# The second layer's M moved into the first attention, and softmax denominators by transposes, in a two-layer graph attention kernel on one core

## The chip, the cores and the metric

The kernel runs on one core of a Trainium2 chip. Its engines, as the profile names them, are PE (TensorE, matmuls and transposes; its weight loads are listed as PEld), DVE (VectorE), ACT (ScalarE), POOL (GpSimd) and SP (SyncE, which here only issues DMAs). The metric is the time of one execution in device microseconds; the time shown for a kernel is a median of its runs. The profile is that of one execution, and its own time is given beside its span.

## The reference, cut to what matters

`x` has 3327 rows of 512 features, `adj` is a 3327 x 3327 matrix of zeros and ones. There are two attention layers, then a layer with binary weights, each closed by a residual and a layer norm:

```
for l in range(2):                      # W_stack[l] is 512 x 1024
    Wh, Ws = split(x @ W_stack[l])
    a = softmax(Wh @ Ws.T) * adj
    x = leaky_relu(a @ Wh + x)
x = layernorm(x0 + x)
out = layernorm(x + relu(adj @ (step(x) @ sign(weight).T)))
```

The scores are `x Wa (x Wb)^T = x (Wa Wb^T) x^T`, where Wa and Wb are the left and the right half of W. The kernel makes the 512 x 512 matrix of the two halves once per layer and calls it M, so that Ws is never formed: queries are x times M, keys are x itself. M depends on the weights alone.

## The kernel before, in words

The 3327 rows are 26 tiles of 128. Two tiles make a half (13 halves, `NQ`), four make a chunk (7 chunks). Large products are done in seven smaller products with sums of operands before and sums of results after (the Strassen and Winograd scheme, `seven`), so each product comes with VectorE, ScalarE and POOL additions. All matmuls are in 32-bit floats, and each shows as two records in the profile.

Each layer has two stages. **`project`** transposes the rows of x, builds M, writes the keys, the values (`ws_d`, with `wh` kept on the chip) and the queries (`gs_d`) with their operand sums to memory. For M it loads the left half of W as `wa` and the right half as `wb`, transposes all sixteen 128 x 128 blocks of each half on TensorE (`pwT`, copied out to `wTs`), and then multiplies them (`pm`, four bands of four matmuls, copied out to `m`). `weave` mixes M's 16 matmuls with the products of the first two value tiles (`wh`). The products for the first queries need M and its sums `msum`.

**`attention`** runs over 169 steps, one for each pair (half of queries `g`, half of keys `q`). In the loop over `v` a step issues, in an order set by fractions from 0 to 1: the scores of 30 steps ahead (`LOOK`, `scores`), the exponentials and running sums of 3 and 2 steps ahead, POOL's operand sums of the masked weights (`sums`, tiles `as`), and the seven value products of step `v` (`values`). The scores of the last chunk have only one half and take less work; from step 152 on no scores are left, and only values are multiplied. After the last step of a half, `finish` adds its parts over the next steps, one per step: `norm` makes the denominators, then residuals and activation follow.

In `norm`, the running total of the exponentials lies with keys on partitions; it is summed over the partitions by a matmul with a column of ones:

```
nc.tensor.matmul(pz[:, i : i + 1], sm[:, ts(i, P)], ones[:, 0:1], start=True, stop=True)
nc.vector.reciprocal(rz, pz)
```

What sets the order: each engine has its own queue and works it in order. Within a stage the order is that in which the program calls the operations; where two stages meet, operations of the next one may be placed between those of the one before. SP's queue holds nearly all loads, in order; POOL's queue holds the stores to memory besides POOL's own sums. Buffers are rings: `slot` gives the next of 33 tiles of 2 KB per partition, used for scores, rows of x, W and operand sums alike; accumulators come from PSUM pools `ps_ch` (3 banks, scores), `ps_acc` (4, values) and `ps_tr` (1, transposes and denominators).

At the start of the second attention `binary_weights` loads the weights of the last layer (`wT`) and makes their signs on VectorE (`neg_w`, `bw`). Their buffers are those of the last rows of x1 (`h`), so the loads wait until these rows are stored. In VectorE's queue they stand among the operations of the second `project`.

Of the kernel before, what the change touches and what calls it, by code (L numbers as in the profile page):

```python
# [9 lines left out]
F32 = mybir.dt.float32  # L10
# [6 lines left out]
AX = mybir.AxisListType  # L17
PSUM = bass.MemoryType.PSUM

P = 128  # L20
# [9 lines left out]
def kernel(  # L30
# [8 lines left out]
    nc = tc.nc  # L39
    N, D = x.shape  # L40
    L = w_stack.shape[0]
    KD = D // P
    HD = D // 2
# [75 lines left out]
    def copy_out(n, dst, src):  # L119
        if n % 2:  # L120
            nc.scalar.copy(dst, src)
        else:
            nc.vector.tensor_copy(dst, src)
# [55 lines left out]
    def left_sums(a11, a12, a21, a22, s1, s2, s3, s4):  # L179
        nc.vector.tensor_tensor(s1, a21, a22, ALU.add)  # L180
        nc.vector.tensor_tensor(s2, s1, a11, ALU.subtract)
        nc.vector.tensor_tensor(s3, a11, a21, ALU.subtract)
        nc.vector.tensor_tensor(s4, a12, s2, ALU.subtract)
# [7 lines left out]
    def weave(*lists):  # L191

        at = [
            ((i + 0.5) / len(part), n, do)
            for n, part in enumerate(lists) for i, do in enumerate(part)
        ]
        for _, _, do in sorted(at, key=lambda e: e[:2]):
            do()

    def project(l, pre):  # L200

        src = x if l == 0 else x1_d
        ch_lane, acc_lane, tr_lane = (ps_ch, "ch"), (ps_acc, "acc"), (ps_tr, "tr")
        xTs, rows_of = {}, {}

        def load_x(c):
# [28 lines left out]
        wb = []  # L235
        for k in range(KD):
            wt = slot([P, D], F32, f"wb_{l}_{k}")
            nc.sync.dma_start(out=wt, in_=w_stack[l, ts(k, P), D:])
            wb.append(wt)
        load_x(1)  # L240
        for k in range(KD):
            transpose_x(0, k, acc_lane)
        wT = {}
        for h in range(2):
            for k in range(KD):
                pool, tag = (acc_lane, ch_lane)[h]
                pt = pool.tile([P, D], F32, tag=tag, name=f"pwT_{l}_{h}_{k}")
                for d in range(KD):
                    of = wa[:, d] if h == 0 else wb[d]
                    nc.tensor.transpose(pt[:, ts(d, P)], of[:, ts(k, P)], ident)  # L250
                wT[h, k] = slot([P, D], F32, f"wTs_{l}_{h}_{k}")
                copy_out(k, wT[h, k], pt)
# [6 lines left out]
        wr = {B11: lo[:, :, :HD], B21: hi[:, :, :HD], B22: hi[:, :, HD:]}  # L259
        wr.update({i: wsum[:, e] for e, i in enumerate((T1, T2, T3, T4))})  # L260
        m = pre.tile([P, KD, D], F32, tag="m", bufs=1, name=f"m_{l}")
        msum = pre.tile([P, 4, 2, HD], F32, tag="msum", bufs=1, name=f"msum_{l}")
        lo, hi = m[:, 0:2], m[:, 2:4]
        ml = {A11: lo[:, :, :HD], A12: hi[:, :, :HD], A21: lo[:, :, HD:], A22: hi[:, :, HD:]}
        ml.update({i: msum[:, e] for e, i in enumerate((S1, S2, S3, S4))})

        def product_m():
            pm = {}

            def one(d, k):  # L270
                if k == 0:
                    pm[d] = ps_acc.tile([P, D], F32, tag="acc", name=f"pm_{l}_{d}")
                nc.tensor.matmul(  # L273
                    pm[d], wT[0, k][:, ts(d, P)], wT[1, k], start=(k == 0), stop=(k == KD - 1)
                )
                if k == KD - 1:
                    copy_out(d, m[:, d], pm[d])

            return [lambda d=d, k=k: one(d, k) for d in range(KD) for k in range(KD)]

        def keys(c, a):

# [128 lines left out]
    def attention(l, att):  # L411
        last = l == L - 1
# [305 lines left out]
        def finish(g):  # L718

            sm = total[g][:, 0]  # L720
            nc.gpsimd.tensor_tensor(sm, sm, total[g][:, 1], ALU.add)
            pz = ps_tr.tile([P, 2], F32, tag="tr", name=f"pz_{l}_{g}")
            rz = small.tile([P, 2], F32, tag="rz", name=f"rz_{l}_{g}")
            hs = out_.pop(g)
            mine = half_tiles(g)
            held = {}

            def norm():
                for i in range(2):
                    nc.tensor.matmul(  # L730
                        pz[:, i : i + 1], sm[:, ts(i, P)], ones[:, 0:1], start=True, stop=True
                    )
# [24 lines left out]
            def sign(i):  # L757

                t, hh = mine[i], hs[i]
                r = rows(t)  # L760
                st = small.tile([P, 6], F32, tag="bn", name=f"bn_{t}")
                nc.vector.bn_stats(st[:r], hh[:r])
                nc.vector.bn_aggr(mv[:r, t, :], st[:r])
                ba = held[i] = att.tile([P, D], BF16, tag="ba", bufs=1, name=f"ba_{t}")
                nc.vector.tensor_scalar(ba[:r], hh[:r], mv[:r, t, 0:1], None, ALU.is_gt)

            def turn(i):
                r = rows(mine[i])
# [24 lines left out]
            if not last:  # L793
                return [norm, lambda: (residual(0), fetch(1)), lambda: None, lambda: residual(1)]
            return [
                norm, lambda: (residual(0), fetch(1)), lambda: sign(0), lambda: turn(0),
                lambda: linear(0), lambda: residual(1), lambda: sign(1), lambda: turn(1),
                lambda: linear(1),
            ]

        if last:
            binary_weights()
        later, after = [], []
        for v in range(-LOOK - 4, len(steps)):
            u = v + LOOK
# [200 lines left out]
```

## Time and profile before

| what | value |
|---|---|
| median of 3 runs | 2721.83 us (2717.41 to 2726.82) |
| the profiled execution, its own time | 2719.29 us |
| its span | 2717.4 us |
| PE, DVE, POOL, ACT busy | 98%, 69%, 48%, 24% of the span |
| mean granted TensorE clock | 0.994 |
| last scores of the first attention end | about 1188 us |
| last value matmul of the first attention ends | 1257.6 us |
| first query product of layer 1 that needs M's sums starts | 1302.22 us |

Times in the profile count from the start of the span. A group of instructions is listed by its source line, its engine, and by what it writes and reads. A line such as "PE a L1 <- DMA b: 2.1, 2, 1.8" in a list of waits says that PE's instructions of line L1, which write a, waited 2.1 us in all, twice, at most 1.8 us, until a DMA into b had landed. In a table of stretches each engine's busy time stands with its number of instructions, then the granted clock as a share of the full one, the busy share of the DMA engines and what they moved.

### The profile page before, as it was taken

The page shows a single profiled execution, that of the slowest core. Times are in us where ns is not written, and L with a number is a line of the kernel's source. Part 1 is how long each engine was busy: PE and PEld are TensorE (multiplying, and loading weights), DVE is VectorE, ACT ScalarE, POOL GpSimd, SP SyncE. Part 2 cuts the span into 40 slices and gives each one's busy share as a digit, 9 for nine tenths or more (in the row PEclk, how much of TensorE's full clock was granted, in tenths as well). Part 3 has the DMA queues.
Part 4 walks back from the last instruction along what each step waited for, and adds up shares of the span by engine and source line. Part 5 has one row for each costly group of instructions (what it writes and reads, how often), then busy time and mean ns, then how long its engine had stood idle before and what let it go on. Part 6 is the DMA issues. An engine that isn't in the chain of part 4 may idle for free.

```text
span 2717.4 us, 38059 instructions
## 1 busy us (share of the span) xinstructions
PE 2651.7 (98%) x12409; PEld 2233.5 (82%) x12409; DVE 1877.1 (69%) x3511; ACT 665.2 (24%) x1571; POOL 1313.6 (48%) x2170
## 2 busy tenths in 40 slices
PE   9999999999999999998999999999999999998997
PEld 6888888888888888876888888888888888877543
DVE  5654777777777777786664667777677777778543
ACT  2323222222222222211332322222222222222100
POOL 2450455555555555775452154545545455566401
PEclk9999999999999999999999999999999999999999
DMA  5765777676777767776665667777777777687882
GB/s 191 258 208 161 237 233 257 226 260 233 257 238 235 260 227 240 254 260 220 235 206 178 206 224 261 239 248 255 238 252 237 275 236 242 235 274 255 286 284 92
DMA packets 280817, 639.54 MB, mean 235 GB/s; under 512 B 35921, under 2 KB 128735, under 8 KB 279078
## 3 DMA queue, kind: packets, MB, share of 16 engines
q1 hardware_dynamic: 244038, 527.32, 58.7%
q0 software_dynamic: 36576, 109.73, 11.0%
q8 instruction: 102, 1.67, 0.2%
q14 instruction: 101, 0.83, 0.1%
HBM read 527.22 MB, written 109.69 MB: 234 GB/s over the span
## 4 chain that ended last, share of the span: by engine, by line
PE 85%; issue 6%; DMA 4%; POOL 3%; DVE 2%; SPq 0%; ACT 0%; POOLq 0%; DVEq 0%; ACTq 0%
PE acc L682 34%; PE pZ L441 19%; PE pY L441 10%; PE pX L441 5%; PE pZ_wh L309 3%; PE pD L441 3%; PE pZ_g L363 3%; DMA ws<-ws_d 2%; PE pY_wh L309 2%; PE pY_g L363 2%; PE pm L273 1%; PE pxw L781 1%; PE pxt L221 1%; PE pX_wh L309 1%; PE pX_g L363 1%
## 5 line engine op out<-in xcount | busy, mean ns | idle before, releaser
L441 PE MATMUL pZ<-gs,xs 128*128 128x256 f32 x2496 | 635.8, 379 | 0.0
L441 PEld LDWEIGHTS pZ<-gs,xs 128*128 128x128 f32 x2496 | 473.6, 190 | 64.8 <-ACT u L458 0.3
L655 POOL TENSOR_TENSOR as<-s 128x128 f32<-128x128 f32 x338 | 168.4, 498 | 734.1 <-DVE s L600 577.1
L682 PE MATMUL acc<-ws,s 128*128 128x256 f32 x1352 | 404.3, 381 | 0.0
L682 PE MATMUL acc<-ws,as 128*128 128x256 f32 x1352 | 352.7, 382 | 30.0 <-DMA ws<-ws_d 17.4
L682 PE MATMUL acc<-wh,s 128*128 128x256 f32 x1352 | 356.9, 380 | 1.7 <-DVE h L706 1.7
L441 PE MATMUL pY<-gs,xs 128*128 128x256 f32 x1248 | 320.3, 379 | 0.0
L511 DVE TENSOR_TENSOR top<-top,s 128x512 f32<-128x512 f32 x312 | 252.7, 810 | 97.8 <-ACT s L493 58.2
L682 PEld LDWEIGHTS acc<-ws,as 128*128 128x128 f32 x1352 | 253.6, 190 | 75.0 <-POOL as L657 12.8
L682 PEld LDWEIGHTS acc<-wh,s 128*128 128x128 f32 x1352 | 258.0, 191 | 37.5 <-DVE h L706 2.1
L682 PEld LDWEIGHTS acc<-ws,s 128*128 128x128 f32 x1352 | 257.3, 191 | 35.1 <-DVE h L714 0.2
L582 DVE TENSOR_TENSOR s<-s,off 128x512 f32<-128x512 f32 x338 | 273.0, 808 | 0.1
L483 DVE TENSOR_TENSOR s<-p,u 128x256 f32<-128x256 f32 x156 | 67.5, 433 | 286.2 <-ACT u L458 285.3
L441 PEld LDWEIGHTS pY<-gs,xs 128*128 128x128 f32 x1248 | 237.0, 190 | 32.3
L585 ACT ACTIVATE s<-s 128x512 f32<-128x512 f32 x338 | 213.7, 632 | 201.5 <-DVE s L582 200.5
L593 DVE TENSOR_TENSOR total<-total,s 128x512 f32<-128x512 f32 x312 | 259.3, 831 | 0.8 <-ACT s L585 0.8
L657 POOL TENSOR_TENSOR as<-s 128x128 f32<-128x128 f32 x338 | 236.5, 700 | 26.5
L600 DVE TENSOR_TENSOR s<-s,adj 128x512 f32<-128x512 f32 (+1 forms) x312 | 226.1, 725 | 5.7
L458 ACT COPY u<-pZ 128x256 f32<-128x256 f32 x312 | 116.4, 373 | 459.9 <-PE pZ L441 459.9
L656 POOL TENSOR_TENSOR s<-s 128x128 f32<-128x128 f32 x338 | 215.2, 637 | 26.5
L658 POOL TENSOR_TENSOR as<-s,as 128x128 f32<-128x128 f32 x338 | 210.5, 623 | 26.5
L682 PE MATMUL acc<-wh,as 128*128 128x256 f32 x676 | 205.8, 386 | 0.0
(185 smaller groups left out, 3501.1 us busy)
## 6 DMA issues: line engine op xcount, KB each, us to landing
ws<-ws_d SPq DMA_DIRECT2D x338, 512.0 KB, 3.9
xs<-xs_d SPq DMA_DIRECT2D x182, 512.0 KB, 5.9
adj<-in_adjT_dram SPq DMA_DIRECT2D x288, 256.0 KB, 4.4
xs<-xs_d SPq DMA_DIRECT2D x156, 384.0 KB, 6.3
gs_d<-gsp POOLq DMA_DIRECT2D x88, 256.0 KB, 3.2
gs<-gs_d SPq DMA_DIRECT2D x12, 1792.0 KB, 11.0
adj_d<-ah POOLq DMA_DIRECT2D x144, 128.0 KB, 4.4
ahl<-adj_d SPq DMA_DIRECT2D x72, 256.0 KB, 4.4
```

The lines of the kernel that those rows point to most:

```text
L309: nc.tensor.matmul(bank, of[LEFT[i]][:, k], wr[RIGHT[i]][:, k], start=(start and k == 0), stop=(k == 1), skip_group_check=True,)
L441: nc.tensor.matmul(ch[bank], xs[c, q, a][:, k], gs[c][:, b, k], start=(start and k == 0), stop=(k == 1), skip_group_check=True,)
L511: nc.vector.tensor_tensor(top[i], top[i], t, ALU.max)
L582: nc.vector.tensor_tensor(s, s, off[g].to_broadcast([P, 2, HW]), ALU.subtract)
L585: nc.scalar.activation(sc[g, q], sc[g, q], AF.Exp)
L593: nc.vector.tensor_tensor(total[g], total[g], sc[g, q], ALU.add)
L600: nc.vector.tensor_tensor(s[:, :, :n], s[:, :, :n], at[:, :, :n], ALU.mult)
L655: nc.gpsimd.tensor_tensor(s3, a11, a21, ALU.subtract)
L656: nc.gpsimd.tensor_tensor(a21, a21, a22, ALU.add)
L657: nc.gpsimd.tensor_tensor(s2, a21, a11, ALU.subtract)
L658: nc.gpsimd.tensor_tensor(s4, a12, s2, ALU.subtract)
L682: nc.tensor.matmul(acc[g][i // 2][:, i % 2], a[i], b[i], start=(q == 0 and i % 2 == 0), stop=(q == NQ - 1), skip_group_check=True,)
```

## The change

For layer 1, W is loaded, transposed and multiplied to M in the last steps of the first attention; layer 0 does as before. Counting steps as `v`: the left half is loaded at step 138 and the right half at 140 into eight slots; in each of the steps 146 to 153 one group of four transposes goes through the `ps_tr` bank and is copied out to a slot; from step 154 to 168 the sixteen matmuls of M run between the value products, in `ps_ch` banks, and are copied out, in turn on VectorE and ScalarE, into two tiles of the ring that held the keys' operands (`xs0`). In the second `project` the left half is still loaded as `wa` for the values; the loads of `wb`, the transposes and M's matmuls are gone. The two value tiles that were woven with M are woven with each other, in `ps_ch` and `ps_acc`. M is copied into its place `m` by two copies on ScalarE, and its sums are made from the tiles of the ring.

In `norm` of both layers the totals are transposed, and the sums are then made by a VectorE reduction along the free axis, and inverted.

```
+    def load_w(l, h):
+        for k in range(KD):
+            w_rows[l, h, k] = slot([P, D], F32, f"w{h}_{l}_{k}")
+            nc.sync.dma_start(out=w_rows[l, h, k], in_=w_stack[l, ts(k, P), ts(h, D)])
+
+    def transpose_w(l, h, k, lane):
+        pool, tag = lane
+        pt = pool.tile([P, D], F32, tag=tag, name=f"pwT_{l}_{h}_{k}")
+        for d in range(KD):
+            nc.tensor.transpose(pt[:, ts(d, P)], w_rows[l, h, d][:, ts(k, P)], ident)
+        wT[l, h, k] = slot([P, D], F32, f"wTs_{l}_{h}_{k}")
+        copy_out(k, wT[l, h, k], pt)
+
+    def product_m(l, lane):
...
+            nc.tensor.matmul(
+                pm[d], wT[l, 0, k][:, ts(d, P)], wT[l, 1, k], start=(k == 0), stop=(k == KD - 1)
+            )
+            if k == KD - 1:
+                copy_out(d, m_of[l][d // 2][:, d % 2], pm[d])
...
-        first, second = (project_values(0, a, ch_lane) for a in range(2))
-        weave(product_m(), first + second)
-        left_sums(*(ml[i] for i in (A11, A12, A21, A22, S1, S2, S3, S4)))
+        if l == 0:
+            first, second = (project_values(0, a, ch_lane) for a in range(2))
+            weave(product_m(l, acc_lane), first + second)
+        else:
+            first, second = (
+                project_values(0, a, lane) for a, lane in enumerate((ch_lane, acc_lane))
+            )
+            weave(first, second)
+            for e in range(2):
+                nc.scalar.copy(m[:, 2 * e : 2 * e + 2], m_of[l][e])
+        of = left(*m_of[l])
+        left_sums(*(of[i] for i in (A11, A12, A21, A22, S1, S2, S3, S4)))
...
-            pz = ps_tr.tile([P, 2], F32, tag="tr", name=f"pz_{l}_{g}")
+            pz = ps_tr.tile([P, 2, P], F32, tag="tr", name=f"pz_{l}_{g}")
...
-                    nc.tensor.matmul(
-                        pz[:, i : i + 1], sm[:, ts(i, P)], ones[:, 0:1], start=True, stop=True
-                    )
-                nc.vector.reciprocal(rz, pz)
+                    nc.tensor.transpose(pz[:, i], sm[:, ts(i, P)], ident)
+                nc.vector.reduce_sum(rz, pz, axis=AX.X)
+                nc.vector.reciprocal(rz, rz)
...
         if last:
             binary_weights()
+        else:
+            end = len(ahead) - LOOK
+            early = {}
+            for h in range(2):
+                early[end - 14 + 2 * h] = [(0.9, lambda h=h: load_w(l + 1, h))]
+                for k in range(KD):
+                    early[end - 6 + KD * h + k] = [
+                        (0.75, lambda h=h, k=k: transpose_w(l + 1, h, k, tr_lane))
+                    ]
...
+            n = len(steps) - end - 2
+            early[end + 2] = [(0.2, begin_m)]
+            for i, do in enumerate(product_m(l + 1, ch_lane)):
+                early.setdefault(end + 2 + i * n // (KD * KD), []).append(
+                    (0.3 + 0.4 * (i % 2), do)
+                )
...
             if v >= 0:
                 work += values(*steps[v])
+            if not last:
+                work += early.get(v, [])
```

More of the change, by code (lines that the diff above doesn't have):

```diff
@@ L198, in weave, with one @@
             do()
+    ch_lane, acc_lane, tr_lane = (ps_ch, "ch"), (ps_acc, "acc"), (ps_tr, "tr")
+    w_rows, wT, m_of = {}, {}, {}
+    def load_w(l, h):
[10 more added lines that the diff above has]
+    def product_m(l, lane):
+        pm = {}
+        def one(d, k):
+            if k == 0:
+                pool, tag = lane
+                pm[d] = pool.tile([P, D], F32, tag=tag, name=f"pm_{l}_{d}")
+            nc.tensor.matmul(
[3 more added lines that the diff above has]
+                copy_out(d, m_of[l][d // 2][:, d % 2], pm[d])
+        return [lambda d=d, k=k: one(d, k) for d in range(KD) for k in range(KD)]
     def project(l, pre):
         src = x if l == 0 else x1_d
-        ch_lane, acc_lane, tr_lane = (ps_ch, "ch"), (ps_acc, "acc"), (ps_tr, "tr")
         xTs, rows_of = {}, {}
@@ L234, in project @@
             nc.sync.dma_start(out=wa[:, k], in_=w_stack[l, ts(k, P), :D])
[L235 to L239, printed above, removed]
+        if l == 0:
+            load_w(l, 1)
+            for k in range(KD):
+                w_rows[l, 0, k] = wa[:, k]
         load_x(1)
@@ L242, in project @@
             transpose_x(0, k, acc_lane)
[L243 to L252, printed above, removed]
+        if l == 0:
+            for h in range(2):
+                for k in range(KD):
+                    transpose_w(l, h, k, (acc_lane, ch_lane)[h])
         wsum = ops.tile([P, 4, 2, HD], F32, tag="gs", name=f"wsum_{l}")
@@ L261, in project, with left @@
         m = pre.tile([P, KD, D], F32, tag="m", bufs=1, name=f"m_{l}")
+        if l == 0:
+            m_of[l] = [m[:, 0:2], m[:, 2:4]]
         msum = pre.tile([P, 4, 2, HD], F32, tag="msum", bufs=1, name=f"msum_{l}")
[L263 to L272, printed above, removed]
-                nc.tensor.matmul(
-                    pm[d], wT[0, k][:, ts(d, P)], wT[1, k], start=(k == 0), stop=(k == KD - 1)
-                )
-                if k == KD - 1:
-                    copy_out(d, m[:, d], pm[d])
-            return [lambda d=d, k=k: one(d, k) for d in range(KD) for k in range(KD)]
+        def left(lo, hi):
+            of = {A11: lo[:, :, :HD], A12: hi[:, :, :HD], A21: lo[:, :, HD:], A22: hi[:, :, HD:]}
+            of.update({i: msum[:, e] for e, i in enumerate((S1, S2, S3, S4))})
+            return of
+        ml = left(m[:, 0:2], m[:, 2:4])
         def keys(c, a):
@@ L379, in queries @@
             return [sums] + one, two + [done]
-        first, second = (project_values(0, a, ch_lane) for a in range(2))
-        weave(product_m(), first + second)
-        left_sums(*(ml[i] for i in (A11, A12, A21, A22, S1, S2, S3, S4)))
+        if l == 0:
+            first, second = (project_values(0, a, ch_lane) for a in range(2))
[9 more added lines that the diff above has]
+        left_sums(*(of[i] for i in (A11, A12, A21, A22, S1, S2, S3, S4)))
         for c in range(NC):
@@ L729, in norm @@
                 for i in range(2):
-                    nc.tensor.matmul(
-                        pz[:, i : i + 1], sm[:, ts(i, P)], ones[:, 0:1], start=True, stop=True
-                    )
-                nc.vector.reciprocal(rz, pz)
+                    nc.tensor.transpose(pz[:, i], sm[:, ts(i, P)], ident)
+                nc.vector.reduce_sum(rz, pz, axis=AX.X)
+                nc.vector.reciprocal(rz, rz)
             def fetch(i):
@@ L802, in attention, with begin_m @@
             binary_weights()
+        else:
+            end = len(ahead) - LOOK
+            early = {}
+            for h in range(2):
+                early[end - 14 + 2 * h] = [(0.9, lambda h=h: load_w(l + 1, h))]
+                for k in range(KD):
+                    early[end - 6 + KD * h + k] = [
+                        (0.75, lambda h=h, k=k: transpose_w(l + 1, h, k, tr_lane))
+                    ]
+            def begin_m():
+                m_of[l + 1] = [
+                    ops.tile([P, 2, D], F32, tag="xs0", name=f"m{e}_{l + 1}") for e in range(2)
+                ]
+            n = len(steps) - end - 2
[4 more added lines that the diff above has]
+                )
         later, after = [], []
```

## The prediction

> **What bounds the kernel now.** I read the page first: its span is 2717.4 us, the profiled execution's own time 2719.29 us, so 1.9 us lie around the span; the median of the three runs, 2721.83 us, stands 2.5 us above that execution. The sum below is made against 2719.3 and carried to 2721.8.
>
> ```profile
> PE 2651.7 (98%) x12409; PEld 2233.5 (82%) x12409; DVE 1877.1 (69%) x3511; ACT 665.2 (24%) x1571; POOL 1313.6 (48%) x2170
> ```
>
> TensorE is the bound on average, but the change works at one place, so next the table of stretches, columns PE, PEld, DVE, ACT, POOL busy, granted clock, DMA share, GB/s. I cut at 1188 (the last scores of the first attention), 1258 (its end) and 1304 (the second projection has got going).
>
> ```profile
> 0.00:1188.00 1188.00, 1177.82 (x5511) 1028.17 (x5512) 837.79 (x1549) 305.15 (x730) 607.41 (x1006) 1.00 0.70 235
> 1188.00:1258.00 70.00, 57.87 (x254) 46.43 (x253) 52.86 (x107) 9.46 (x16) 55.00 (x86) 0.98 0.69 223
> 1258.00:1304.00 46.00, 40.01 (x162) 28.03 (x163) 29.58 (x60) 9.53 (x21) 11.87 (x19) 0.93 0.62 216
> 1304.00:2640.00 1336.00, 1313.12 (x6197) 1101.56 (x6198) 926.01 (x1724) 338.10 (x792) 631.98 (x1046) 1.00 0.73 244
> ```
>
> The first and fourth stretches are TensorE without holes: what is taken off TensorE there is time. In the second it idles 12.1 us. The waits of PE from 1188 to 1258 (in all us, times, longest):
>
> ```profile
> PE acc L682 <- POOL as L657: 9.6, 7, 3.2
> PE acc L682 <- DVE h L706: 1.7, 1, 1.7
> ```
>
> and from 1258 to 1304:
>
> ```profile
> PE pwT L250 <- DMA wa<-in_w_stack_dram: 2.1, 2, 1.8
> PE pZ_wh L309 <- DVE s L181: 1.4, 1, 1.4
> PE pwT L250 <- DMA wb<-in_w_stack_dram: 1.0, 1, 1.0
> PE pZ_g L363 <- DVE xt L187: 0.9, 1, 0.9
> PE pxt L221 <- DVE xT L123: 0.6, 1, 0.6
> ```
>
> So the tail of the first attention (steps 152 to 168, values without scores) waits for POOL's sums of the weights: a step costs 3.03 us of matmuls but comes every 3.9 to 4.1 us. In POOL's timeline from 1192 to 1256 one instruction follows the other, but for 3.0 us at 1242.8 and under 2 us of short gaps. Then the transition: W loads, 32 transposes, M, values, all in series.
>
> **What the Trainium skill says.** "SBUF — State Buffer", Who interferes with whom: a VectorE instruction with two SBUF inputs contends with a GpSimd one that reads SBUF; one with at most one SBUF input outside the two-port modes does not, and a reduce never does. The trace agrees on the first: POOL's 128x128 sums take 0.45 us while VectorE is idle and 0.78 beside its adds. The moved copies and the new reduce read PSUM, so I charge POOL nothing. "TensorE: Matmul & The Clock Gate", What's actually happening: after an idle window of about 3.4 us the clock halves. Here the stretch 1250–1275 has clock 0.86, and its 13 last W transposes took 3.12 us where 13 earlier took 2.18.
>
> **The change, part by part.** Times are relative to E, the end of the last value matmul, 1257.6 before.
>
> 1. Denominators. From the timeline of PE (start, us, x records):
>
> ```profile
> 376.94 0.50 PE L730 MATMUL pz<-ones,total 128*128 128x1 f32 x4
> 377.30 0.68 PE L682 MATMUL acc<-wh,as 128*128 128x256 f32 x2
> 377.82 0.59 PE L682 MATMUL acc<-ws,s 128*128 128x256 f32 x2
> ...
> 1189.70 0.38 PE L543 MATMUL ptop<-ident,top 128*128 128x128 f32 x2
> 1189.92 0.60 PE L682 MATMUL acc<-ws,as 128*128 128x256 f32 x2
> ```
>
> From 376.94 to 377.82 pass 0.88 us for the pz records and one pair that costs 0.43: pz takes 0.44. Two transposes take 0.22 (1189.70 to 1189.92). Gain 0.22 each; 11 of the 13 in each layer lie in TensorE-bound steps: −2.4 us in layer 0, −2.4 in layer 1. VectorE gains a reduce of 128x256 from PSUM, 0.42 us as ptop's (L546), hidden under 70% busy; without that cover it costs 26 × 0.42 = 10.9.
>
> 2. Eight loads of W (256 KB each) on SP's queue, four at step 138, four at 140, ahead of the next ws, adj and xs loads. Each waits for the DMA eight places back and for score copies some eight steps old, so SP isn't held. The first four x1 row loads of layer 1 move about three steps back in the same queue and are still some 14 steps early; POOL's queue is passed by nothing. Transfers: around there a step of 4.75 us moves about 243 GB/s, and peaks of 369 are seen, so 0.6 MB per step is free; 1 MB leaves 0.4 MB, 1.1 us, before the next ws load. ws lands in 3.6/4.2/5.7 us (min/median/max) and is needed 6.2 us after its issue. Cost 0, bound 2.
>
> 3. 32 transposes, one group of four in each of steps 146 to 153. A group costs 0.43 us; 146 to 151 are TensorE-bound (4.75 us a step, no hole): 6 × 0.43 = +2.6. The groups of 152 and 153 fall where POOL has a lead. All pass through the only tr bank: poff at step 152 comes behind a VectorE copy (0.69), about 1 us on off, while POOL reaches those sums 2.9 us after they are ready. Cost 0, bound 1.
>
> 4. M's 16 matmuls, two records each with 0.43 between starts, 0.86 us, in steps 154 to 168: 13.8 us on TensorE against 12.1 us of holes; per step 3.03 + 0.92 = 3.95, just POOL's pace. POOL's "as" tiles have three buffers, so its step and TensorE's overlap. Following POOL's times of before from step 166 (1248.22): 166 ends at 1251.2, 167 with one M matmul at 1255.1, 168 has its sums at 1255.33 and ends, with the last M matmul, at 1259.0: +1.4. Two M copies and two wT copies join VectorE's queue (0.69 each); the M copies stand ahead of the shift of a later step, wait for TensorE, and POOL's sums wait behind; slack there is 1.2 us, 1 to 2 us come in: +0.5, bound 0 to 3. E moves by −2.4 + 2.6 + 1.4 + 0.5 = +2.1.
>
> 5. The transition. Removed: 32 transposes, 8 copies, 16 matmuls, 1 MB of W right-half loads. Kept: wa and wsum. Added: two ScalarE copies of M, 128x1024. Price: "VectorE: DVE Perf Modes", TRN2 errata, gives ScalarE 224 + elements cycles at 1.2 GHz, an estimate of 1.04 us; the exponentials of 512 by the same rule 0.61, measured 0.633. Before, the first query product that needs msum and xt starts at 1302.22 = E + 44.6. After, TensorE: wa lands at about E + 4, values start, stall once for wsum and keys (E + 8.5), end by E + 17.6; the first M copy delays the first query to E + 19.3; with four query products and one transpose group it stands before msum at E + 23.2. VectorE's queue is longer: take-outs to 1.1, reduce, xT copies, residuals and wsum (0.6 each) to 7.7, eight key sums (0.34) to 10.5, two adds to 11.2. Then come the binary weights (neg_w, bw), which stay on VectorE and wait (VectorE's waits from 1258 to 1304):
>
> ```profile
> DVE neg_w L406 <- DMA wT<-in_weightT_dram: 3.0, 2, 2.1
> ```
>
> The wT loads wait for the stores of the last x1 rows (issued about E + 5.4, 4.7 us to landing as a median, 6.1 to 9.1 at this place), then 2.8 us: first at 13.2 to 14.8, third only after the first bw: 17.1 to 18.8. Adds, bw and t sums stand behind; t ends at 23.6 to 25.2, msum and xt (six at 0.62) at 27.4 to 29.1. I take 28. TensorE then idles 4.8 us, long enough for the half clock: +1.2. So E + 29.2 against E + 44.6: −15.4. Where the stall goes: from W loads to VectorE's binary weights. Behind that product the order is the same as before.
>
> Sum: −2.4 + 2.6 + 1.9 − 15.4 − 2.4 = −15.7. 2719.3 − 15.7 = 2703.6; on the median 2706.
>
> **Rivals.** B: VectorE isn't late (x1 stores land fast, clock stays): the product starts at E + 23.2, another −6.0: 2700. For it: the 1 MB of loads that slowed those stores is gone. Against: the third wT load still waits for the first bw. C: the tail hides nothing, M's 13.8 us all come on E instead of 1.4: +12.4, 2718.5, the same as before. For it: 13.8 us into 12.1 us of holes, and VectorE, POOL and TensorE wait for each other in a ring. Against: the three buffers. D, slower: the clock gate, in the tail. There TensorE gets 45.5 + 13.8 = 59.3 us of work; a share of it that runs at half clock takes twice its time, and no hole is left to take it. It turns the gain of 15.7 into a loss of over 8 once it adds 24 us, that is from 40% of the tail on; with 50% it adds 29.7 and gives 2736. For it: a patch of slow matmuls stands at 1205–1209 before, after holes of 1.7 and 0.5, and "TensorE: Matmul & The Clock Gate", Part 4, says that transposes don't keep the clock up. Against: the granted clock is 0.98 over the tail with holes of up to 3.2, the change fills holes, and only two groups of transposes lie there. F: the transposes with a sum don't help (the reduce's latency eats it): 4.8 us less, 2711.
>
> **How the numbers follow.** Chances: forecast 0.58, B 0.12, F 0.10, C 0.14, D 0.06. 0.3% is 8.2 us, about what a measurement of this kernel can tell from no change. Faster by more: 0.55 of the forecast, 0.12 of B, 0.10 of F: 0.77. Same: C with 0.13 and 0.03 of the forecast: 0.16. Slower: D and a rest of C: 0.07. The forecast's own range: better by 3 if POOL's hole of 3.0 at 1242.8 doesn't come back and by 2 from early stores, worse by 3 (tail copies), 2 (burst of loads), 1 (tr bank), 1: 2701 to 2713. With B, F and the near half of C: 2698 to 2717.
>
> **What would show it.** Right: pz pairs of 0.22; no holes in steps 138 to 151; PE's wait for "as" in the tail mostly gone and the end of the values at about 1259.7; no wait for wb; neg_w's wait for wT grown, and a PE wait of some 5 us on xt before the query products. Wrong: waits for ws near step 139 or 141; tail steps over 4.5 us; the query products at E + 23; a clock under 0.9 in the tail.

## The result and the profile after

The changed kernel takes 2706.90 us as a median of five runs (2704.40 to 2711.31); the kernel before, in the same comparison, 2719.62 us (2716.64 to 2726.82). The ratio is 0.9951 with a 95% interval of 0.9933 to 0.9970, which is 8 to 18 us less. The forecast was 2706, in a range of 2698 to 2717. The profiled execution of the changed kernel is the slowest of its five: its own time is 2711.31 us, its span 2709.5 us, so the two profiled executions differ by 8.0 us where the medians differ by 12.7.

The page of the changed kernel, busy time by engine:

```profile
PE 2642.3 (98%) x12332; PEld 2225.7 (82%) x12357; DVE 1884.0 (70%) x3537; ACT 666.5 (25%) x1573; POOL 1312.7 (48%) x2170
```

TensorE is busy 9.4 us less. Only some 6 us of that are work, the 52 records of pz that are gone; 25 more matmul records are missing from this trace, as the count beside PEld's shows. M is the same work in another place. The table of stretches, cut at the same times as before (columns PE, PEld, DVE, ACT, POOL busy, granted clock, DMA share, GB/s), shows where it went:

```profile
0.00:1188.00 1188.00, 1176.24 (x5505) 1026.01 (x5506) 842.67 (x1562) 305.66 (x731) 600.50 (x1005) 1.00 0.70 236
1188.00:1258.00 70.00, 66.36 (x282) 51.03 (x281) 53.20 (x106) 11.10 (x19) 54.95 (x88) 1.00 0.71 225
1258.00:1304.00 46.00, 35.93 (x167) 29.15 (x166) 32.77 (x70) 13.01 (x29) 13.60 (x23) 0.93 0.60 207
1304.00:2640.00 1336.00, 1308.81 (x6128) 1093.80 (x6152) 926.96 (x1731) 333.78 (x782) 636.59 (x1044) 0.99 0.73 246
```

In the second stretch TensorE is busy 66.4 of 70 us in place of 57.9: M went into the holes. The granted clock there is 1.00. In the third it is *less* busy than before, 35.9 of 46 us: the work left, and a new wait came. TensorE's waits from 1188 to 1258:

```profile
PE acc L708 <- POOL as L683: 2.6, 2, 1.8
PE poff L579 <- DVE wTs L123: 0.5, 1, 0.5
PE pz L756 <- POOL total L747: 0.3, 1, 0.3
PE acc L708 <- DMA ws<-ws_d: 0.3, 1, 0.3
```

and from 1258 to 1304:

```profile
PE pZ_g L380 <- DVE xt L187: 5.7, 1, 5.7
PE pZ_wh L326 <- DVE s L181: 1.7, 2, 1.3
PE pZ_g L380 <- ACT m L407: 1.4, 1, 1.4
PE pZ_wh L326 <- DMA wa<-in_w_stack_dram: 0.7, 1, 0.7
PE pX_wh L326 <- DMA wa<-in_w_stack_dram: 0.6, 1, 0.6
```

The waits for wb and for transposed W are gone; one wait of 5.7 us stands in their place, for `xt`, which is VectorE. What held VectorE is in its own list of waits over the same stretch:

```profile
DVE neg_w L432 <- DMA wT<-in_weightT_dram: 5.5, 2, 2.8
```

This is the chain that the prediction describes: binary weights wait for their loads, and M's sums and the query operand sums stand behind them. In TensorE's timeline (start, us, instruction, idle time before it and what ended it):

```profile
1280.88 1.13 PE L380 MATMUL pZ_g<-xT,m 128*128 128x256 f32 x4 [1.41 <-ACT m L407]
...
1283.15 1.89 PE L380 MATMUL pX_g<-xT,m 128*128 128x256 f32 x8
1290.77 2.05 PE L380 MATMUL pZ_g<-xt,msum 128*128 128x256 f32 x4 [5.73 <-DVE xt L187]
```

The last value product ends at 1261.10 (1257.59 before), so the first product with M's sums comes 29.7 us after it, in place of 44.6. Its first four records take 1.83 us to the next start where 0.86 is the rule: the half clock behind the wait, which was forecast. From 1290.77 to 1294.2 the granted clock is 0.50. The product's eight records and the group of transposes among them are through at 1294.71, 3.94 us after its start; where no wait stands before it, in e8, the same work takes 2.16. So the half clock costs 1.8 us, behind the product's start.

The denominators, in TensorE's timeline at the same place as before:

```profile
377.44 0.38 PE L756 MATMUL pz<-ident,total 128*128 128x128 f32 x2
377.66 0.60 PE L708 MATMUL acc<-wh,as 128*128 128x256 f32 x2
```

Two transposes hold TensorE for 0.22 us (0.44 before). To see where along the run time is won and lost, take the start of the exponentials of each step in ScalarE's timeline, changed kernel minus before: +0.5 at the first step, then a drop of 0.2 every thirteen steps to −2.6 at step 143, −2.3 at 144, +2.1 at 154, +2.3 at 168. With the points above: +3.5 at the end of the values, −11.5 at the first product with M's sums. In the second attention −10.6 at its first step, −9.1 at its last, −8.0 at the end.

### The profile page after: what moved, and what is told of

The parts are those of the page before. It is cut to its first block, busy times and chain, and to the rows that moved or that the text cites. A ratio compares the mean times of both kernels' runs of the same rounds, so it can differ in the third digit from the quotient of the medians.

```text
span 2709.5 us, 37972 instructions
## 1 busy us (share of the span) xinstructions
PE 2642.3 (98%) x12332; PEld 2225.7 (82%) x12357; DVE 1884.0 (70%) x3537; ACT 666.5 (25%) x1573; POOL 1312.7 (48%) x2170
## 4 chain that ended last, share of the span: by engine, by line
PE 84%; issue 6%; DMA 4%; DVE 3%; POOL 3%; SPq 0%; ACT 0%; POOLq 0%; DVEq 0%; ACTq 0%
PE acc L708 34%; PE pZ L467 19%; PE pY L467 10%; PE pX L467 5%; PE pZ_g L380 3%; PE pZ_wh L326 3%; PE pD L467 3%; DMA ws<-ws_d 2%; PE pY_wh L326 2%; PE pY_g L380 2%; PE pm L225 1%; PE pX_wh L326 1%; PE pxw L806 1%; PE pxt L253 1%; PE pX_g L380 1%
## 5 line engine op out<-in xcount | busy, mean ns | idle before, releaser
L681 POOL TENSOR_TENSOR as<-s 128x128 f32<-128x128 f32 x338 | 168.1, 497 | 742.6 <-DVE s L626 580.7
L683 POOL TENSOR_TENSOR as<-s 128x128 f32<-128x128 f32 x338 | 230.6, 682 | 26.5
```

Source lines behind the costliest of these rows:

```text
L681: nc.gpsimd.tensor_tensor(s3, a11, a21, ALU.subtract)
L683: nc.gpsimd.tensor_tensor(s2, a21, a11, ALU.subtract)
```

## The experiments

"E" is the end of the last value product of the first attention in the profiled execution, read as the start of what TensorE does next; "product" is the first query product of layer 1 with M's sums. Each ratio is against the kernel before on the same chip (medians there 2718.7 to 2720.0). e1 to e4, e5 to e8 and e9 to e11 each shared a chip, so a difference between rows of different groups carries about a microsecond more of doubt than its medians show.

| run | median us | ratio, 95% interval | E | product − E |
|---|---|---|---|---|
| before | 2719.62 | | 1257.6 | 44.6 |
| changed kernel | 2706.90 | 0.9951 (0.9933–0.9970) | 1261.1 | 29.7 |
| e1 denominators alone | 2718.05 | 0.9992 (0.9983–1.0001) | 1256.2 | 48.0 |
| e2 M alone | 2710.68 | 0.9964 (0.9952–0.9976) | 1263.2 | 28.7 |
| e3 changed, binary weights early | 2700.46 | 0.9928 (0.9914–0.9942) | 1262.0 | 25.6 |
| e4 changed, M's matmuls back | 2712.49 | 0.9972 (0.9961–0.9983) | 1261.4 | 37.4 |
| e5 before, binary weights early | 2719.81 | 0.9999 (0.9991–1.0008) | 1259.4 | 42.5 |
| e6 e5 with the denominators | 2711.54 | 0.9969 (0.9957–0.9981) | 1256.1 | 41.6 |
| e7 changed, sums first | 2704.77 | 0.9943 (0.9929–0.9956) | 1263.7 | 24.7 |
| e8 e3 and e7 together | 2698.39 | 0.9920 (0.9906–0.9933) | 1262.1 | 22.0 |
| e9 changed, M twice | 2716.43 | 0.9990 (0.9984–0.9997) | 1271.6 | 28.8 |
| e10 before, filler in the tail | 2720.08 | 1.0005 (0.9999–1.0012) | 1260.4 | 45.9 |
| e11 e8, loads of W spread | 2695.89 | 0.9914 (0.9901–0.9928) | 1259.7 | 22.0 |

### e1 and e2: the two parts apart

e1 is the kernel before with the new `norm`:

```
...
-                    nc.tensor.matmul(
-                        pz[:, i : i + 1], sm[:, ts(i, P)], ones[:, 0:1], start=True, stop=True
-                    )
-                nc.vector.reciprocal(rz, pz)
+                    nc.tensor.transpose(pz[:, i], sm[:, ts(i, P)], ident)
+                nc.vector.reduce_sum(rz, pz, axis=AX.X)
+                nc.vector.reciprocal(rz, rz)
```

> The kernel before with the new denominators alone (two transposes and a sum along the free axis). My theory: each of the 26 denominators gives back 0.22 us of TensorE where TensorE is the bound, 11 in each layer, so the exponentials of step 140 of the first layer come 2.4 us earlier than before (2.4 to 3.1 as the profile of the changed kernel hints), and 4.8 us in all, about 2715 against 2719.6. Rival F (the reduction's latency eats it): nothing, 2719.6. A third reading, from the second layer of the changed kernel's profile: the steps there also give 0.2 each but waits for the loads of ws take it back, then 2.4 to 3 in all, 2717.

Measured: 2718.05 us, 2.0 less than before, with zero inside the interval. The steps do what was priced: the exponentials start +1.1 us against before at the first step and −1.6 at step 154, 2.7 us won. It is lost right after. E is 1.4 us earlier, but the product comes at 1304.21 in place of 1302.22. TensorE's waits of e1 from 1253 to 1306, first line:

```profile
PE pZ_wh L309 <- DVE s L181: 4.9, 1, 4.9
```

and VectorE's from 1256 to 1306:

```profile
DVE neg_w L406 <- DMA wT<-in_weightT_dram: 4.9, 1, 4.9
```

Before, these two waits were 1.4 and 3.0. In the kernel before the first of the binary weights stands in VectorE's queue between the sums of W, so the key sums wait with it. Coming earlier doesn't help in this execution: the load of wT is issued when the rows of x1 are stored, and in e1 these stores landed later. The transfers from 1250 to 1275, before:

```profile
x_d<-h POOLq DMA_DIRECT2D x1, 256.0 KB, 6.2
```

and in e1:

```profile
x_d<-h POOLq DMA_DIRECT2D x1, 256.0 KB, 7.7
```

wT's first use is at 1272.06 before and at 1272.36 in e1, so the wait ends where it ended before, 0.3 us later. The other 1.7 us come behind it:

```profile
1276.01 2.00 PE L309 MATMUL pZ_wh<-wsum,s 128*128 128x256 f32 x4 [4.94 <-DVE s L181]
1277.80 1.85 PE L273 MATMUL pm<-wTs,wTs 128*128 128x512 f32 x2
```

These six records take 3.48 us to the next start and before, at the same place, 1.80: the granted clock is 0.50 from 1276.1 to 1279.4. So a gain ahead of this point ended in a longer wait, and the longer wait in a stretch at half clock. That this holds in every execution of e1 isn't shown, only in the profiled one.

e2 is the changed kernel with the old `norm` (the diff above, reversed).

> The changed kernel with the old denominators (a matmul with a column of ones). My theory: everything but the two times 2.4 us stays, so 2719.6 - 10.9 = 2708.7, and the first query product with M's sums still comes 29 to 30 us after the last value product. If the denominators give nothing (rival F), the time of the changed kernel, 2706.9.

Measured: 2710.68 us, 3.8 more than the changed kernel, nearer to the 4.8 of the theory than to the nothing of rival F (by the ratios, each against its own chip, 3.4); the product comes 28.7 us after E. With M moved the denominators give 3.8 us, alone 2.0; the intervals don't separate the two figures, nor the sum of the parts from the whole. The two parts alone add to 2.0 + 9.3 = 11.3 us, against 12.7 for both.

### e5 and e6: the denominators without the chain

e5 makes the binary weights in the first attention, in the kernel before, and e6 adds the denominators:

```
...
-        if last:
-            binary_weights()
+        early = {}
+        if not last:
+            for k in range(KD):
+                early[4 * NQ + 5 + k] = [(0.9, lambda k=k: binary_weights(k))]
...
+            work += early.get(v, [])
```

> The kernel before with the binary weights made at steps 57 to 60 of the first attention, nothing else. It serves as the base for the next run. TensorE's waits after the first attention that VectorE or the loads of the binary weights can explain are 1.4 us for the key sums, 0.9 for the query operand sums and 0.6 for xT: 2 to 3 us less than before, 2717 to 2718, if the loads of the binary weights hold the transition there too; no change if they don't.

> As the run before it, with the new denominators too. The denominators alone gave 2.0 us where 4.8 were expected; in their profile the first attention's steps come 2.7 us earlier in relation to the first step, and the first query product with M's sums comes no earlier, since a wait of 4.9 us for the loads of the binary weights stood in VectorE's queue. Theory: those loads take the first layer's part back; with them away the denominators give all of it, 4.8 us less than the base (4 to 5). Rival: the denominators are worth only 2 us in themselves: 2 us less than the base.

Measured: e5 2719.81 (no change), e6 2711.54, 8.3 us less than e5; from the two intervals, 4 to 12. The denominators are worth more than 2 us once the binary weights are away: the rival falls. Why it is more than 4.8 stays open; the interval reaches down to 4. The two profiled executions differ by 7.1 us: 2.2 are won before step 144, where the theory has 2.4, 2.0 from there to the product and 2.9 behind it. In the middle part e5 has more half clock than e6 (granted from 1188 to 1258: 0.90 against 0.95). In e6's profile TensorE's waits after the first attention hold no `s` at all (from 1253 to 1306):

```profile
PE pwT L250 <- DMA wa<-in_w_stack_dram: 2.4, 4, 1.5
PE pZ_g L363 <- DVE xt L187: 0.9, 1, 0.9
PE pxt L221 <- DVE xT L123: 0.6, 1, 0.6
PE pwT L250 <- ACT wTs L121: 0.2, 1, 0.2
```

e5's expected 2 to 3 us didn't show as a time, though the product does come 2.1 us sooner after E. In its profiled execution E itself is 1.8 us later, and the timeline of TensorE says why. e5:

```profile
1248.33 2.08 PE L682 MATMUL acc<-ws,as 128*128 128x256 f32 x4 [3.17 <-POOL as L657]
1250.20 1.06 PE L682 MATMUL acc<-ws,s 128*128 128x256 f32 x2
1251.05 1.06 PE L682 MATMUL acc<-wh,as 128*128 128x256 f32 x2
```

and before, at the same instruction:

```profile
1248.22 1.13 PE L682 MATMUL acc<-ws,as 128*128 128x256 f32 x4 [3.16 <-POOL as L657]
1249.19 0.59 PE L682 MATMUL acc<-ws,s 128*128 128x256 f32 x2
```

The same wait of 3.2 us is followed by half speed in one execution and not in the other. The stretch from 1247.2 to 1254 (granted clock: the third figure from the end), e5 and then before:

```profile
1247.20:1254.00 6.80, 5.67 (x13) 4.56 (x14) 1.27 (x8) 0.00 (x0) 5.77 (x13) 0.50 0.13 32
1247.20:1254.00 6.80, 5.78 (x27) 5.11 (x28) 1.17 (x8) 0.00 (x0) 5.79 (x13) 1.00 0.39 119
```

### e3, e7 and e8: what holds the product

e3 moves the binary weights to steps 57 to 60 of the first attention in the changed kernel (the diff of e5, put into its `early`).

> The changed kernel with the binary weights (four loads, eight VectorE instructions) made at steps 57 to 60 of the first attention, one a step. My theory (VectorE, held by the loads of the binary weights, sets the first query product with M's sums): the value tiles' sums end some 5 us earlier, and the product starts about 24 us after the last value product in place of 29.7; the 3.8 us of VectorE are hidden at steps 57 to 60. 5.5 us less than the changed kernel and 1 more where the half clock after the long wait goes: 2700 to 2702. Rival: VectorE's own work between (48 instructions, some 24 us) sets it and the waits only filled slack: under 2 us less, 2705 to 2707.

Measured: 2700.46 us, 6.4 less than the changed kernel. The product comes 25.6 us after E; no wait for xt is left before it. TensorE's waits from 1258 to 1304:

```profile
PE pZ_wh L326 <- DVE s L181: 3.2, 2, 2.9
PE pZ_g L380 <- ACT m L407: 1.4, 1, 1.4
PE pxt L253 <- DVE xT L123: 0.6, 1, 0.6
```

So the binary weights, 5.5 us of waits for their loads and 3.8 us of their own instructions, held the product, and not the rest of VectorE's work. e3 moves the loads and the instructions together, so it doesn't tell their shares. e7 leaves them and moves what stood behind them:

```
...
-            weave(first, second)
-            for e in range(2):
-                nc.scalar.copy(m[:, 2 * e : 2 * e + 2], m_of[l][e])
-        of = left(*m_of[l])
-        left_sums(*(of[i] for i in (A11, A12, A21, A22, S1, S2, S3, S4)))
+            for n in range(8):
+                first[n]()
+                second[n]()
+                if n == 0:
+                    m_sums()
+                    for e in range(2):
+                        nc.scalar.copy(m[:, 2 * e : 2 * e + 2], m_of[l][e])
...
+                one, two = queries(c, (ch_lane, acc_lane))
+                if l:
+                    one.pop(0)()
+                    first[8]()
+                    second[8]()
+                weave(one, two, turns)
```

> The changed kernel with M's sums (four VectorE instructions), M's copies and the query operand sums ahead of the value tiles' sums in their queues; the binary weights stay where they are. Theory (the product is late because its operands' sums stand behind other work in VectorE's queue): TensorE no longer waits 1.4 us for M's copy; the operand sums still stand behind the fourth binary weight, about 21 us after the last value product, so the product starts at 24 (29.7 in the changed kernel) and the kernel takes 2700 to 2702. Rival: what is taken off the product's wait comes back behind it, because the value sums that stand last now hold the key and query sums of the next chunk: 2705 or more.

Measured: 2704.77 us, between the two. The product comes at E + 24.7, as the theory has it, but the kernel gains only 2.1. TensorE's waits from 1262 to 1304, first two lines:

```profile
PE pxt L253 <- DVE xT L123: 2.7, 1, 2.7
PE pZ_g L380 <- DVE xt L187: 2.5, 1, 2.5
```

The wait for `xt` has become shorter, and a new one stands behind it: the value sums, now last in VectorE's queue, hold the copy that frees the only bank for transposes. At the product e7's profile stood 13.8 us ahead of before, at the first step of the second attention 10.3; behind the 2.7 us of that wait the granted clock is 0.50 from 1294.1 to 1297.4. The rival was right on the mechanism: with the loads still in the queue, a reorder passes the wait on.

e8 does both.

> The changed kernel with the binary weights at steps 57 to 60 and with M's sums, M's copies and the query operand sums ahead of the value tiles' sums. Theory: TensorE alone sets the first query product with M's sums: values end about 18.5 us after the last value product of the attention, four query products and one group of transposes follow, so 22 to 23 us, no wait for xt, no half clock: 2697 to 2699, 8 to 10 below the changed kernel. Rival: the moves share one cause and don't add, 2700 to 2701 as the binary weights' move alone.

Measured: 2698.39 us, 8.5 below the changed kernel, inside the theory's range. TensorE's waits from 1258 to 1304:

```profile
PE pZ_wh L326 <- DVE s L181: 2.1, 2, 1.7
PE pZ_wh L326 <- DVE rz L770: 0.2, 1, 0.2
PE pZ_wh L326 <- DMA wa<-in_w_stack_dram: 0.2, 1, 0.2
```

No wait stands between the values and the queries; the product comes 22.0 us after E and there is no half clock: its eight records take 1.72 us to the next start.

### e4, e9 and e10: what the tail hides

e4 weaves M's matmuls with the values of the second projection as the kernel before did; loads and transposes of W stay in the first attention.

```
...
-            for i, do in enumerate(product_m(l + 1, ch_lane)):
-                early.setdefault(end + 2 + i * n // (KD * KD), []).append(
-                    (0.3 + 0.4 * (i % 2), do)
-                )
...
-            weave(first, second)
+            weave(product_m(l, acc_lane), first + second)
```

> The changed kernel with M's sixteen matmuls and four copies moved back into the second projection, woven with the first two value tiles as before; loads and transposes stay in the first attention. My theory (the waits for POOL's sums hide nearly all of M in the tail): the last value product comes only 2 to 3 us earlier, and the first query product with M's sums comes 37 us after it in place of 29.7, so 4 to 6 us more than the changed kernel: 2711 to 2713. Rival C (the tail hides nothing): the last value product comes 13.8 us earlier, and the kernel is 6 us faster than the changed one: 2701.

Measured: 2712.49 us, 5.6 more than the changed kernel, as the theory has it; rival C wanted 6 less. The product comes 37.4 us after E. But E, at 1261.4, came no earlier than in the changed kernel, where 2 to 3 us were expected: in the profiled execution two waits for ws (1.35 us at 1142.6 and 2.14 at 1205.6) stand against that, and two stretches at half clock behind waits for POOL (granted 0.50 from 1234.3 to 1237.7 and from 1251.4 to 1254.8), which the changed kernel's tail doesn't have. From the exponentials of step 144 to E the time added against before is 5.1 us in e4 and 5.8 in the changed kernel, so by this count M's sixteen matmuls in the tail cost at least 0.7 us; the waits for ws and the half clock in e4 hide some more.

e9 gives the tail sixteen matmuls more: each band of M is multiplied a second time before it is copied out.

```
...
             if k == KD - 1:
+                for j in range(KD if l else 0):
+                    nc.tensor.matmul(
+                        pm[d], wT[l, 0, j][:, ts(d, P)], wT[l, 1, j], start=(j == 0), stop=(j == KD - 1)
+                    )
                 copy_out(d, m_of[l][d // 2][:, d % 2], pm[d])
```

> The changed kernel with each of the four bands of M multiplied twice in the tail: sixteen more matmuls of 0.86 us, 13.8 us of TensorE, nothing else. Theory: the first sixteen used up the tail's holes (12.1 us before, some 3 to 4 us left), so of these 10 to 12 us come on the end of the values: 2717 to 2719. Rival: POOL's sums still set the pace of the tail and hide more: 7 us or less, 2714 or less.

Measured: 2716.43 us, 9.5 more than the changed kernel; E is 10.5 us later. Of 13.8 us added, 10.5 are paid, where of the first 13.8 about 1 was. The tail of e9 in the table of stretches and in TensorE's waits, 1188 to 1258:

```profile
1188.00:1258.00 70.00, 68.92 (x277) 50.30 (x276) 52.02 (x103) 11.01 (x19) 50.65 (x80) 1.00 0.63 203
```

```profile
PE acc L712 <- DMA ws<-ws_d: 0.5, 1, 0.5
PE poff L583 <- DVE wTs L123: 0.5, 1, 0.5
```

No wait for POOL is left: TensorE is the bound, and the cover is spent. M fits the holes, and little more does.

e10 puts filler into the tail of the kernel before, to see what the filling itself does:

```
...
+            def fill():
+                nc.tensor.matmul(
+                    warm["p"], ident, wh[0][:, 0], start=True, stop=True
+                )
...
+            for v in range(end + 2, len(steps)):
+                warm.setdefault(v, []).extend([(0.3, fill), (0.7, fill)])
```

> The kernel before with two unused matmuls of 128x256 (0.43 us each) in each tail step, 34 in all, 14.6 us of TensorE; nothing of the change. They fill holes as M's matmuls do. Theory: their own cost at the end of the values is 1 to 2 us, as M's was; but a run of matmuls at half clock behind a wait (0.9 us at 1205.8 in the profile before, 1.8 us behind the 3.2 us wait at 1248 in the profile of the run with the binary weights moved) goes away, so the median stays within 1.5 us of before, and the executions lie closer together: under 6 us from the fastest to the slowest (10.7 before). Rival: the spread of the kernel before has nothing to do with the tail: median 1 to 2 us slower, spread as before.

Measured: 2720.08 us against 2718.71, and the 21 executions lie between 2716.2 and 2724.5. E moved 1.2 us in relation to the steps before the tail, so the cost of filling was right. The half speed behind the wait at 1205.8 is gone, but the executions are hardly closer together (8.3 us, and 10.0 for before in the same comparison). What I expected of the spread is wrong: it doesn't come from the tail, or not from it alone. What makes it stays open. What filling does to the clock shows across the profiles: from 1188 to 1258 the granted clock is 0.90 to 0.98 in all five kernels whose tail isn't filled (before, e1, e4, e5, e6) and 1.00 in all eight that have M or filler there.

### e11: the loads of W

```
...
-                early[end - 14 + 2 * h] = [(0.9, lambda h=h: load_w(l + 1, h))]
+                for k in range(KD):
+                    early[end - 16 + KD * h + k] = [(0.9, lambda h=h, k=k: load_w(l + 1, h, (k,)))]
```

> The kernel of the binary weights and the sums moved, with the eight loads of W one a step at steps 136 to 143 in place of four at 138 and four at 140. Theory: the waits for ws of 0.3 and 0.6 us that stand at steps 139 and 141 in the changed kernel come from these bursts and go: 0 to 1 us less than that kernel, 2697.5 to 2698.4, not measurable as a time, to be read from TensorE's waits between 1110 and 1160. Rival: these waits are scatter of the loads of ws: they stay.

In the changed kernel TensorE's waits from 1100 to 1188 are:

```profile
PE acc L708 <- DMA ws<-ws_d: 0.9, 2, 0.6
```

They stand at 1130.5 and 1140.9, one step behind each burst of four loads. In e11, as before, this stretch has no wait at all, though as much is moved there: from 1130 to 1150, first the changed kernel,

```profile
1130.00:1150.00 20.00, 19.11 (x90) 16.35 (x88) 13.97 (x33) 3.65 (x8) 11.61 (x21) 1.00 0.91 308
```

and e11:

```profile
1130.00:1150.00 20.00, 20.00 (x95) 17.57 (x95) 15.80 (x34) 4.38 (x9) 12.41 (x21) 1.00 0.92 314
```

DMA is 91 to 92% busy in both. What differs is the order, 1 MB in front of a load that is needed 6 us later. The other profiles agree: all seven kernels with the bursts wait for ws in this stretch (0.5 us in e8 to 2.7 in e7), the six without them don't. As a time, 2695.89 against 2698.39 isn't separated by the intervals. e11 is the fastest kernel here: 23 us below the kernel before, 11 below the changed one.

## Why the prediction was right, step by step

**Step 1, denominators (−2.4 and −2.4).** The price was right: 0.22 us each. The first attention gained 3.1 us up to step 143: drops of 0.2 at each denominator, together 2.2, one of 0.6 at step 24 that isn't theirs (e2, with the old denominators, shows it too), and smaller ones. The second shows the same drops, but in the profiled execution waits took them back: it was 10.6 us ahead at its first step and 9.1 at its last. Its waits from 1304 to 2640 that differ from before most:

```profile
PE acc L708 <- DMA ws<-ws_d: 15.0, 12, 4.5
PE acc L708 <- POOL total L747: 3.1, 1, 3.1
PE acc L708 <- POOL as L683: 2.6, 1, 2.6
```

Before, ws stood there with 17.0 us and these two with none. The granted clock took a little too: 0.94 from 2420 to 2560, where before had 0.96 from 2430 to 2570. What the prediction didn't see is that this gain depends on what stands behind it: alone, it ended in the wait for the binary weights and the half clock after it (e1; without that wait, e6).

**Step 2, loads of W (0, bound 2).** Mis-sized: 0.9 us here, inside the bound, but 2.7 in e7, outside it; spread over the steps they cost nothing (e11). The sum lets 1.1 us of a burst stand before the next ws load and has it land in time. The ws loads issued right behind the two bursts took 6.6 and 6.9 us to land, those of before in this stretch 3.6 to 5.7. Waits for ws at steps 139 and 141 were named as a sign of being wrong: they came, but small.

**Step 3, transposes (+2.6).** Mis-sized. The prediction let the groups of steps 152 and 153 go free, because POOL has a lead there. All eight cost TensorE their 0.43, 3.4 us, and the copy of a group held the only transpose bank for 0.5 us before poff, inside the bound set for that: 3.9 together. In those two steps TensorE went on without a wait but that one, so POOL's lead wasn't there to hide them.

**Step 4, M in the tail (+1.9).** What remains to E is +0.5 from the start of the run, −3.1 + 0.9 + 3.9, and about +1.3 for M: together the measured +3.5. M's part is a remainder. Counted directly, from the first product of step 154 to E, TensorE takes 62.54 us before and 63.46 now, 0.9 more. The waits for POOL fell from 10.1 to 2.6 us. e4 and e9 fit this: at least 0.7 us for the first sixteen matmuls, 10.5 for the next. Two readings of the prediction are rough here without a change to the sum: POOL's short gaps come to 2.7 us, not under 2, and its pace of 3.9 to 4.1 us a step is a mean (single steps of before lie 3.0 to 6.5 us apart, and some of the changed kernel pass the 4.5 that was named as a sign of being wrong). Rival C is out, and so is D: the clock in the tail is 1.00.

**Step 5, the transition (−15.4).** The forecast has the product start at E + 28 and adds 1.2 us for the half clock, which falls behind that start: 29.2 in all. Measured, the product starts at E + 29.7, so it is the start that came 1.7 us late, and 15.0 are won there. For the product's eight records and the transposes among them the changed kernel takes 3.94 us and before, with a wait of 0.6 for xT in it, 3.08, so 0.9 are lost again: −14.1 for −15.4. The stall is where it was put: 5.5 us of VectorE's waits for wT, 5.7 us of TensorE's for xt (4.8 forecast), the half clock behind it. e3 shows that it is the binary weights. The price of M's copies, an estimate of 1.04 us from "VectorE: DVE Perf Modes", TRN2 errata, is met: 1.05.

**The sum.** E was to move by +2.1 and moved by +3.5; the transition gave 14.1 for 15.4; so the second attention starts 10.6 us ahead where 13.3 were forecast. From there the second layer's −2.4 didn't come, and 2.6 more went into waits and half clock of that one execution. Own time against own time this gives −8.0 in place of −15.7, and −12.7 on the medians, which hold four quicker executions. The mechanism was right where the sum is large, in the tail and in the transition; that 2706.90 lies so near 2706 is partly luck, since the gain was 3.0 us smaller than forecast and the kernel before measured 2.2 us less than the median that the forecast started from. Rival B (VectorE not late) is what e8 makes true: the product at E + 22.0 where B had E + 23.2, and 8.5 us where B had 6.0, the wait of 1.4 us for M's copy having gone too. Rival F isn't borne out with M moved (e2) or with the binary weights away (e6), but without them e1 can't be told from no change.

## What to carry to other kernels

Find the stretch in which the bound engine waits for another one, and put independent work of the next stage there; price it against the sum of those waits, since most of the next portion of the same size is paid (10.5 of 13.8 us in e9). Before you count a gain as time, look one stage ahead for a load that is tied to a late store and stands in a queue in front of other work: it can take the gain back. Moving such a load gave nothing by itself (e5), but some 6 us where the denominators were in (e6 against e1) and as much on top of the whole change (e3). Hand loads that aren't urgent to the queue one a step, behind the one that is.

## What the runs showed of the hardware

A wait of TensorE of 3.16 us was followed by full speed and one of 3.17 us, at the same instruction in another execution, by matmuls of twice the time for 5.7 us (e5); the end of the values came 1.8 us later. At this place the five kernels with an unfilled tail wait 3.0 to 3.2 us for POOL's sums; half speed followed in three (e4, e5, e6) and not in two (before, e1). In the kernel before, waits of 1.7 and 0.5 us close together led to half speed at 1205.8. "TensorE: Matmul & The Clock Gate", What's actually happening, in the Trainium skill says that the window is free-running, so that where it lies against a wait is a matter of chance; that would fit these runs, but none tests it, and the waits here are shorter than the 3.4 us that the page gives for the idle window. From the first 15 us on and up to 2640 us, every stretch at half clock in these traces lasts 3.4 us or two or three times that.

A 32-bit matmul of a single column took TensorE 0.22 us, half of one of 256 columns (0.43), and twice a transpose of 128 (0.11): four records with four weight loads for two of the first, two with two for two of the last.
